# A graph-attention and hypergraph kernel on one core: a second buffer for the transposed adjacency, one transpose placed earlier on VectorE, two prologue vectors in borrowed buffers

## The chip, the core and the metric

The kernel runs on one core of one Trainium2 chip. The time is the device time of one execution in microseconds (us). The core has a matrix engine (TensorE, PE in the profile; the loading of its weights has a row of its own, PEld), a vector engine (VectorE, DVE), a scalar engine (ScalarE, ACT), a general engine (GpSimd, POOL) and an engine that issues transfers (SyncE, SP). [...]

## What is computed

There are 128 graphs of 128 nodes with 512 features each, all in fp32. Layer 0 is graph attention with 8 heads, then a residual and a layer norm. Layer 1 is two hypergraph convolutions with a ReLU and a layer norm between them, then residuals and a layer norm. Cut to what matters here:

```python
# layer 0: attention, 8 heads of 64
feats = einsum('bnf,hfu->bhnu', X, W)
dense = leaky_relu(e_self[..., :, None] + e_neigh[..., None, :], 0.2)
dense = dense + NEG_BIG * (1.0 - A[:, None])
out   = relu(softmax(dense) @ feats + b)
x     = layernorm(x + out)
# layer 1: two hypergraph convolutions (w1 512->1024, w2 1024->512)
def hypergraph_conv(x, adj, W, b):
    H  = (adj != 0)
    Dn = 1 / (H @ adj[first row]);  Be = 1 / H.sum(axis=1)
    m  = Be * (H^T @ (x @ W^T))
    return Dn * (H @ m) + b
h = layer_norm(relu(hypergraph_conv(x, adj, W1, b1)))
x = layernorm(x + hypergraph_conv(h, adj, W2, b2) + x)
```

## The kernel before

**Tiling.** Two graphs make a pair, and 64 pairs are worked through. Everything of a pair lies with the 128 nodes or 128 features across the partitions. The propagator `R`, the product H·Be·H^T scaled by Dn, is made once for each graph (`propagator`, L432, into the PSUM tile `pd`; `r_evict`, L440) and used in both convolutions. The large products are done by a scheme with seven products instead of eight, so TensorE's results of one product are added to others by VectorE and ScalarE: `chain` lists the products in the order 1, 2, 6, 5, 7, 4, 3. They go into three PSUM banks: X, Y and W. Product 5 opens bank W; VectorE's `y_sum` then adds a copy of X to W; and only after that may product 3 add into the same bank W. For the second weights this is `pyX`, `pyY`, `pyW` (multiplied at L476), the sums are L924, and ScalarE's copies of X are L332. For the first weights the names are `phX`, `phY`, `phW` (L840), with sums at L855.

**Pipeline.** A pair passes through stages that are spread over five periods ("lags" 0 to 4). In one period TensorE works at the second convolution of one pair, the features and attention of another, and the first convolution of a third. The period is 38.6 units in the planner's reckoning. Each function carries a lag and a due time; all functions of all pairs are sorted by `(pair + lag) * 38.6 + due` and written out in that order, which becomes the order on every engine's queue. So a due time is only a place in a queue, not a time at which anything runs.

**VectorE's order around the change.** In this stretch of a period VectorE's queue holds, with due times: `attended_pair` (26.3, L724 and L725, attention results to `y`), `sum_blocks` (28.9, L939 to L944, sums for the middle layer norm), `residual` of graph 0 (29.0, L739, `y <- max(y,0)+x`, then its statistics L747 and L748), `y_sum` for bank Y (30.6, L924), `residual` of graph 1 (30.7), `rstds` (30.8, L753), `x_transpose` of graph 1 (30.85, L373), `y_sum` for bank W (33.9, L924 again), `edges` (35.75, L409 to L416), `largest` (36.1, L601), a further `y_sum` on bank W (0.1 of the next period), `r_evict` (L440). GpSimd adds the bias to `y` ahead of the residuals (`add_bias`, L730, two instructions), takes the reciprocal root after `rstds` (L755), and masks the scores (L579). ScalarE then normalizes `y` (`first_output`, L782), which TensorE multiplies by `R` (`propagate`, L805, tile `pz`); ScalarE copies that out (`z_evict`, L817, tile `zT`).

**`x_transpose`** turns 32 x 32 blocks of a pair's x, loaded blockwise as `xb` by four transfers, into `xT`, one instruction for each graph (the first half due 26.15, the second 30.85). `xT` is read by the feature products in the following period.

**`edges`** transposes the adjacency blocks `ab` into `hT`, compares with zero and counts degrees. `hT` is one buffer: `edges` of pair p stands in the queues ahead of `propagator` of pair p-1, which still reads `hT` of pair p-1, so the first instruction of `edges` waits for that product:

```python
hT = work.tile([P, 2, N], F32, tag="hT", name=f"hT_{p}")   # one buffer
@step(0, 35.75)   # edges, of pair p
@step(1, 40.1)    # propagator, of pair p - 1: 1.5 units into the next period
```

**Prologue.** The attention vectors `as_bc` and `an_bc` are spread over the partitions by two transfers from ScalarE's queue at the very start and read by `prepare_first` (L222). The tag `eb` holds two larger buffers for the exponentials on their way to the transpose (`e_read`, L621).

Of the kernel before, what the change touches and what calls it, by code (L numbers as in the profile page):

```python
# [8 lines left out]
F32 = mybir.dt.float32  # L9
# [11 lines left out]
def kernel(  # L21
# [46 lines left out]
    G, N, F = x.shape  # L68
    P = 128
# [13 lines left out]
    const = ctx.enter_context(tc.tile_pool(name="const", bufs=1))  # L83
    work = ctx.enter_context(tc.tile_pool(name="work", bufs=1))
# [72 lines left out]
    def everywhere(t, ap, queue):  # L157
        queue.dma_start(t, ap.partition_broadcast(P))

    as_bc, an_bc, b0_bc, b2_bc, bw_bc = (  # L160
        const.tile([P, F], F32, name=n) for n in ("as_bc", "an_bc", "b0_bc", "b2_bc", "bw_bc")
    )

    vecs = const.tile([P, 3, KH], F32, name="vecs")
# [139 lines left out]
    def step(lag, time, since=0, until=PAIRS):  # L304

        def keep(fn):
            steps.append((lag, time, fn.__name__, range(since, until), fn, ()))
            return fn
        return keep

    def at(lag, time, fn, *args, since=0, until=PAIRS):
        steps.append((lag, time, fn.__name__, range(since, until), fn, args))
# [63 lines left out]
        )  # L376

    at(0, 26.15, x_transpose, 0, since=2)
    at(0, 30.85, x_transpose, 1, since=2)

    def x_transpose_first(p, s):
        s["px"] = [bank(f"px_{p}_{g}") for g in range(2)]
# [17 lines left out]
    @step(0, 35.75)  # L400
    def edges(p, s):

        deg = small.tile([P, 2], F32, tag="deg", name=f"deg_{p}")
        hT = work.tile([P, 2, N], F32, tag="hT", name=f"hT_{p}")
        if p < 2:
            src = s["pt"][:, :2 * N].rearrange("p (g n) -> p g n", g=2)
        else:
            src = hT
            nc.vector.transpose(hT.rearrange("p g (b n) -> p (g b) n", b=NB), s["ab"])  # L409
        for g in range(2):  # L410
            nc.vector.tensor_scalar(
                hT[:, g, :], src[:, g, :], 0.0, None, op0=ALU.not_equal, op1=ALU.add,
                accum_out=deg[:, g:g + 1],
            )
        nc.vector.tensor_scalar(deg, deg, 1.0, None, op0=ALU.max)
        nc.vector.reciprocal(deg, deg)  # L416
        s["hT"], s["be"] = hT, deg
# [65 lines left out]
    def feature(s, i, to, start):  # L483
# [4 lines left out]
          feature, FW, since=2)  # L488
# [772 lines left out]
```

## Time and profile before

| quantity | value |
|---|---|
| time, median of 3 runs | 2449.46 us (2448.19 to 2449.68) |
| span of the profiled execution | 2448.5 us |
| TensorE matmul / weight loads busy | 2419.9 us / 2146.3 us |
| VectorE, ScalarE, GpSimd busy | 1906.3, 1528.1, 1803.8 us |
| HBM traffic | 239.08 MB read, 102.73 MB written |

The page gives each engine's busy time, then the chain that ended last, then groups of instructions by line with the idle time just ahead of them and what ended it. Idle time of an engine matters only if somebody whom the end depends on waits behind it.

A timeline lists instructions in order of their start: start, duration, engine, line, operation, output and inputs, shapes, count, and in brackets the idle time before it and what ended that. Several like instructions are merged in one line; durations on TensorE overlap, so the distance between two starts is the better measure there. TensorE's work of a period, from one `pd` to the next, takes about 37.4 us.

### The profile page before, as it was taken

Reading aid. Unit: us, or ns where it says so; the run is one execution under the profiler, and the core shown is the slowest. Engines: PE = TensorE matmul, PEld = TensorE weight load, DVE = VectorE, ACT = ScalarE, POOL = GpSimd, SP = SyncE. Lnnn points to the kernel's source line nnn. Section 1 sums busy time; section 2 is a strip of 40 time slices with the busy share of each in tenths; the row PEclk is TensorE's granted clock in tenths of the full one; section 3 lists DMA queues with packets and bytes.
Section 4 is the critical chain, followed back from the end, with each engine's and each line's share of the span. In section 5 each row is a group of like instructions: output and inputs, shape, how many; then the busy total and the mean of one; then the engine's idle time right before and its main releaser. Section 6 shows DMA issues by size and latency. Waiting matters only on the chain.

```text
span 2448.5 us, 52709 instructions
## 1 busy us (share of the span) xinstructions
PE 2419.9 (99%) x18273; PEld 2146.3 (88%) x18273; DVE 1906.3 (78%) x4456; ACT 1528.1 (62%) x4481; POOL 1803.8 (74%) x2060
## 2 busy tenths in 40 slices
PE   7999999999999999999999999999999999999998
PEld 5888888888888888888888888888888888888897
DVE  7877778778778777787787787777877877877776
ACT  4665765756756657657567566576575675665763
POOL 5777776777777777777777777777777777777774
PEclk9999999999999999999999999999999999999999
DMA  6545445445455454454454554554544545545531
GB/s 184 138 139 151 144 132 150 144 134 148 140 144 147 136 154 140 135 151 142 135 145 145 142 147 140 149 148 129 153 136 139 150 139 147 144 138 152 144 112 52
DMA packets 432762, 345.30 MB, mean 141 GB/s; under 512 B 153176, under 2 KB 382064, under 8 KB 432496
## 3 DMA queue, kind: packets, MB, share of 16 engines
q1 hardware_dynamic: 429024, 337.46, 48.4%
q10 hardware_dynamic: 3472, 4.47, 0.5%
q8 instruction: 145, 2.38, 0.4%
q14 instruction: 121, 0.99, 0.1%
HBM read 239.08 MB, written 102.73 MB: 140 GB/s over the span
## 4 chain that ended last, share of the span: by engine, by line
PE 96%; DVE 2%; DMA 1%; ACT 1%; issue 0%; POOL 0%; SPq 0%; POOLq 0%; DVEq 0%; ACTq 0%
PE phX L840 19%; PE pyX L476 18%; PE pyW L476 9%; PE phW L840 9%; PE pfX L476 9%; PE pav L693 5%; PE pz L805 5%; PE phY L840 5%; PE pfW L476 4%; PE pq L1006 4%; PE pyY L476 4%; PE pfY L476 2%; PE pd L432 1%; PE pf L513 1%; PE py L1052 0%
## 5 line engine op out<-in xcount | busy, mean ns | idle before, releaser
L332 ACT COPY py<-pyX 128x257 f32<-128x257 f32 x189 | 70.8, 375 | 531.2 <-PE pyX L476 526.7
L840 PEld LDWEIGHTS phX<-zS,w_sb 128*128 128x128 f32 x3072 | 362.8, 192 | 41.3 <-issue 31.4
L840 PE MATMUL phX<-zS,w_sb 128*128 128x128 f32 x3072 | 378.8, 276 | 2.2 <-POOL xS L458 1.3
L893 POOL TENSOR_TENSOR sq<-sq 128x512 f32<-128x512 f32 (+2 forms) x384 | 329.6, 858 | 20.3 <-ACT sq L881 0.3
L579 POOL TENSOR_TENSOR nb<-nb,neg 128x512 f32<-128x512 f32 x256 | 318.0, 1275 | 7.5 <-DMA nb<-rd 7.3
L595 ACT ACTIVATE nb<-nb,ft 128x128 f32<-128x128 f32 x1020 | 317.3, 390 | 6.8 <-POOL nb L579 6.8
L755 POOL TENSOR_TENSOR rso<-veo,mhalf 128x2 f32<-128x2 f32 x63 | 44.2, 702 | 372.4 <-DVE veo L753 372.4
L609 ACT ACTIVATE nb<-nb,nm 128x128 f32<-128x128 f32 x1024 | 313.8, 394 | 0.4 <-DVE nm L601 0.4
L870 ACT ACTIVATE h<-h,vecs 128x128 f32<-128x128 f32 x768 | 245.5, 395 | 29.7 <-DVE h L855 29.7
L476 PE MATMUL pyW<-w_sb,hS 128*128 128x256 f32 x1008 | 243.9, 384 | 2.5 <-DVE y L924 2.2
L476 PE MATMUL pyX<-w_sb,hS 128*128 128x257 f32 x1008 | 245.6, 385 | 0.0
L476 PE MATMUL pyX<-w_sb,h 128*128 128x257 f32 x1008 | 239.2, 379 | 0.5 <-ACT py L332 0.5
L409 DVE STREAM_TRANSPOSE hT<-ab 128x256 f32<-128x256 f32 x62 | 27.6, 445 | 264.2 <-PE pd L432 264.2
L476 PEld LDWEIGHTS pyW<-w_sb,hS 128*128 128x128 f32 x1008 | 186.2, 189 | 44.1 <-issue 17.7
L476 PEld LDWEIGHTS pyX<-w_sb,h 128*128 128x128 f32 x1008 | 190.9, 190 | 29.0 <-ACT py L332 0.9
L476 PEld LDWEIGHTS pyX<-w_sb,hS 128*128 128x128 f32 x1008 | 185.8, 189 | 28.7
L499 DVE TENSOR_TENSOR ft<-pf,pfW 128x264 f32<-128x264 f32 x124 | 53.2, 429 | 170.3 <-PE pfW L476 89.4
L601 DVE TENSOR_REDUCE nm<-nb 128x4 f32<-128x512 f32 x256 | 169.2, 681 | 7.0 <-ACT nb L595 6.0
L630 DVE STREAM_TRANSPOSE eT<-eb 128x512 f32<-128x512 f32 x252 | 163.5, 687 | 0.6 <-DMA eb<-ed 0.5
L881 ACT ACTIVATE sq<-h 128x512 f32<-128x512 f32 x256 | 160.4, 627 | 2.1
L730 POOL TENSOR_TENSOR y<-y,b_bc 128x512 f32<-128x512 f32 x128 | 160.1, 1272 | 1.9 <-DVE y L704 1.5
L458 POOL TENSOR_TENSOR hS<-h 128x512 f32<-128x512 f32 x126 | 158.9, 1282 | 2.3 <-ACT h L870 2.3
(178 smaller groups left out, 5810.3 us busy)
## 6 DMA issues: line engine op xcount, KB each, us to landing
nb<-rd SPq DMA_DIRECT2D x127, 512.0 KB
ed<-nb SPq DMA_DIRECT2D x126, 512.0 KB
eb<-ed SPq DMA_DIRECT2D x504, 128.0 KB
x<-in_x_dram SPq DMA_DIRECT2D x64, 512.0 KB
out_dram<-o SPq DMA_DIRECT2D x63, 512.0 KB
xb<-in_x_dram SPq DMA_DIRECT2D x248, 128.0 KB
a<-in_adj_dram SPq DMA_DIRECT2D x64, 128.0 KB
w<-in_adj_dram SPq DMA_DIRECT2D x128, 64.0 KB
```

The source lines that it names most:

```text
L458: engine.tensor_tensor(t[:, i], in0, in1, op=op)
L476: nc.tensor.matmul(to[:, :n], lhs[:, k, :], rhs[:, k, :n], start=bool(start) and k == 0, stop=(k == nk - 1), skip_group_check=True,)
L579: nc.gpsimd.tensor_tensor(t, t, neg[:, :, None, :].to_broadcast([P, NB, HH, B]), op=ALU.add)
L595: nc.scalar.activation(t, t, AF.Prelu, bias=s["ft"][:, g, h, 0:1], alpha=SLOPE)
L601: nc.vector.tensor_reduce(s["nm"][:, g, hs], scores(p, s, g, hs).rearrange("p b h j -> p h b j"), AX.XY, ALU.max, negate=True,)
L609: nc.scalar.activation(t, t, AF.Exp, bias=s["nm"][:, g, h:h + 1])
L630: nc.vector.transpose(s["eT"][:, g, hs, :].rearrange("p h (b i) -> p h b i", b=NB), s["eb", g][:, :, hs, :].rearrange("p b h j -> p h b j"),)
L730: nc.gpsimd.tensor_tensor(s["y"][:, g, :], s["y"][:, g, :], b0_bc, op=ALU.add)
L840: nc.tensor.matmul(to[:, m * N:(m + 1) * N], w[:, k, m * P:(m + 1) * P], rhs[:, k, :], start=bool(start) and m == 0 and k == 0, stop=(k == ...
L870: nc.scalar.activation(dst[:, k, :], src[:, k, :], AF.Relu, bias=b1_sb[:, c:c + 1])
L881: nc.scalar.activation(s["sq"][:, g, q * KH // 2:(q + 1) * KH // 2, :], hid(s, g, q), AF.Square, scale=DH ** -0.5,)
L893: nc.gpsimd.tensor_tensor(t[:, :n, :], t[:, :n, :], t[:, n:2 * n, :], op=ALU.add)
```

## The change

The tag `hT` gets two buffers. The second half of `x_transpose` gets the due time 28.95 instead of 30.85. This puts it behind `sum_blocks` and ahead of both `residual` functions instead of behind `rstds`. For pair 2 an explicit table sets both transposes' places, which stay as they were; for pairs 0 and 1 another function makes `xT`. The vectors `as_bc` and `an_bc` are taken from the tag `eb` in the pool `work` instead of having buffers of their own in `const`.

```diff
-    as_bc, an_bc, b0_bc, b2_bc, bw_bc = (
-        const.tile([P, F], F32, name=n) for n in ("as_bc", "an_bc", "b0_bc", "b2_bc", "bw_bc")
+    as_bc, an_bc = (
+        work.tile([P, F], F32, tag="eb", name=n, bufs=2) for n in ("as_bc", "an_bc")
+    )
+    b0_bc, b2_bc, bw_bc = (
+        const.tile([P, F], F32, name=n) for n in ("b0_bc", "b2_bc", "bw_bc")
     )
...
     at(0, 26.15, x_transpose, 0, since=2)
-    at(0, 30.85, x_transpose, 1, since=2)
+    at(0, 28.95, x_transpose, 1, since=2)
...
-        hT = work.tile([P, 2, N], F32, tag="hT", name=f"hT_{p}")
+        hT = work.tile([P, 2, N], F32, tag="hT", name=f"hT_{p}", bufs=2)
```

In the order of the built programs, no instruction is added or removed on any engine. On VectorE the second `x_transpose` stands ahead of eight instructions (L739, L747, L748, L924, L739, L747, L748, L753) that it followed before, once per period; the transpose into `hT` (L409) no longer carries a wait on TensorE; the next `y_sum` on bank W and `r_evict` (L440) carry it instead, each for its own input. The orders on GpSimd, ScalarE, TensorE and SyncE are the same; on TensorE one wait on its own earlier work stands at the first `pfY` product instead of the first `pfX`.

## The prediction

> **What bounds the kernel now.** I read the busy times and the chain of waits first.
>
> ```profile
> PE 2419.9 (99%) x18273; PEld 2146.3 (88%) x18273; DVE 1906.3 (78%) x4456; ACT 1528.1 (62%) x4481; POOL 1803.8 (74%) x2060
> PE 96%; DVE 2%; DMA 1%; ACT 1%; issue 0%; POOL 0%; SPq 0%; POOLq 0%; DVEq 0%; ACTq 0%
> ```
>
> TensorE sets the end; from one `pd` to the next it takes a median 37.39 us. An edit on VectorE is worth only what it takes out of TensorE's row. Next, the waits, VectorE's and TensorE's:
>
> ```profile
> DVE hT L409 <- PE pd L432: 264.2, 61, 4.4
> PEld pyW L476 <- issue: 17.7, 61, 0.5
> PE pyW L476 <- DVE y L924: 2.2, 2, 2.0
> ```
>
> The largest wait (4.3 us a period) is the one for the single `hT` buffer, but it is VectorE's own. The second row is small, unexplained ("issue") and regular: 61 times, 0.29 us, before a weight load for `pyW`. The third names VectorE's L924 at that place. So I read one period there, TensorE and then VectorE:
>
> ```profile
> 1211.79 1.89 PE L476 MATMUL pyW<-w_sb,hS 128*128 128x256 f32 x8
> 1213.52 1.89 PE L476 MATMUL pyX<-w_sb,h 128*128 128x256 f32 x8
> 1215.33 1.97 PE L476 MATMUL pyW<-w_sb,hS 128*128 128x256 f32 x8
> 1217.14 1.95 PE L805 MATMUL pz<-R,y 128*128 128x128 f32 x16
> ...
> 1209.36 1.51 DVE L739 SCALAR_TENSOR_TENSOR y<-y,x 128x512 f32<-128x512 f32 x1
> 1210.90 0.69 DVE L747 BATCH_NORM_STATS2 statsa<-y 128x6 f32<-128x512 f32 x1
> 1212.04 0.69 DVE L739 SCALAR_TENSOR_TENSOR y<-y,x 128x512 f32<-128x512 f32 x1
> 1213.70 0.17 DVE L753 TENSOR_SCALAR vea<-mva 128x2 f32<-128x2 f32 x1
> 1213.78 1.11 DVE L373 STREAM_TRANSPOSE xT<-xb 128x512 f32<-128x512 f32 x1
> 1214.80 0.39 DVE L924 TENSOR_TENSOR y<-py,pyW 128x256 f32<-128x256 f32 x1
> 1219.57 0.45 DVE L409 STREAM_TRANSPOSE hT<-ab 128x256 f32<-128x256 f32 x1 [4.38 <-PE pd L432]
> ```
>
> Groups of eight `py` products start 1.73 us apart (1211.79 to 1213.52); the next two distances are 1.81 and 1.81. L924 ends at 1215.19 and the weights of the last `pyW` group load at 1215.30: product 3 adds into the bank that L924 still reads. L373, the transpose that the change moves, stands right ahead of that L924. The last period with this pattern has no L373, since there is no further pair:
>
> ```profile
> 2372.99 1.89 PE L476 MATMUL pyX<-w_sb,h 128*128 128x256 f32 x8
> 2374.72 1.89 PE L476 MATMUL pyW<-w_sb,hS 128*128 128x256 f32 x8
> 2376.45 1.95 PE L805 MATMUL pz<-R,y 128*128 128x128 f32 x16
> ...
> 2373.26 0.42 DVE L924 TENSOR_TENSOR y<-py,pyW 128x256 f32<-128x256 f32 x1 [0.51 <-PE pyW L476]
> ```
>
> There both distances are 1.73 and the period is 37.25 us. The second 0.075 us belongs to the same wait: a weight load that waited no longer overlaps the products before it.
>
> [...] 99% busy hides the 0.14 us a period above. [...] the first L739 (two inputs) takes 1.51 us beside GpSimd's second L730, which ends at 1210.33; the second L739 takes 0.69; L373 (one input) takes 1.15 beside GpSimd and 1.09 elsewhere. [...] after a stop of some 2.2 us at 89 to 91 us the `pz` products lie 0.213 us apart, not 0.11.
>
> **The change, part by part.**
>
> *The transpose ahead of the residuals.* L373 issues no DMA and goes ahead of eight VectorE instructions. It starts at 1209.36; its follower starts 1.02 us later (1213.78 to 1214.80), at 1210.38. By then L730 has ended (1210.33), so the first L739 takes 0.69 us and its follower starts at 1210.38 + 0.72 = 1211.10, against 1210.90: everything from there to L753 is 0.20 us later, because the transpose fills the time in which the residual was held. L924 follows L753 at once: 1213.98 to 1214.37. With the 0.11 us seen above, TensorE could load at 1214.48; it wants to at 1213.52 + 1.73 - 0.21 = 1215.04. Margin 0.56 us, so the wait goes. In the 60 periods from 96.6 us on that have L373, the first distances sum to 4.6 us more than 60 x 1.731 and the second to 4.5 more than 60 x 1.732 (three periods lose 0.2 to 0.3 extra, within the margin). Gain 9.1 us.
>
> *What is queued behind the 0.20 us.* GpSimd's L755, ScalarE's L773 to L782. L782 for graph 0 ends 1215.88 + 0.20 = 1216.08; `pz` loads at 1216.93 - 0.14 = 1216.79. ScalarE's copies then end at 1218.21, the first `zT` copy starts there, the second is due when `pz` is done, 1219.12 - 0.14 = 1218.98, and ScalarE is free for it at 1218.69. GpSimd's four L579 end about 0.2 later, and `zS` has over 1 us before its product. All of this lies beside TensorE: cost zero.
>
> *The first such period (54 to 97 us)* lacks margin: the groups at 87.46, 91.35 and 93.84 us take 3.89, 2.49 and 2.75 us instead of 1.73, 1.73 and 1.78. VectorE reaches L739 only at 85.18, and L924 ends at 91.21. With the transpose first L739 waits for L730's end (86.38) as before, and L924 comes 0.99 us earlier. At least 0.97 us is won; if the shorter stop does not drop the clock, another 0.69 + 0.96, so 2.6. Stops of 1.1 and 1.3 us at 61 to 64 us left the clock up. ScalarE then limits it: L922 ends at 94.07, so its second `zT` copy can start 0.48 us later, at about 94.5 instead of 96.79. I take 2.1.
>
> *Two buffers for `hT`.* VectorE's 61 waits, 264.2 us, go. TensorE gains nothing by it: behind L409 stand L601, L924, L440, L963 and L855, whose results TensorE needs at 1228.4 at the earliest (L996 ends at 1226.37). L924 and L440 now wait on TensorE for `pyW` and `pd`, some 2 us earlier than they run now. Queued behind them are L963, whose input transfers are issued from 1216.31 to 1218.89, and L601 and L855, which need ScalarE and `phY` at 1223; nobody gets later. The `ab` transfers are issued until 1203.3; their landing is not shown, but a late one would be hidden until 1219.57. Bounds: nothing below, since VectorE takes the same order earlier; above, 0.21 us a period if the other regular loss moved (the `ph` groups at 1224.73 and 1226.65 take 1.92 and 1.86 us for 1.79). I take 0: that one waits for ScalarE's copy L332 at 1225.94, ahead of which ScalarE is busy without a break from its second `zT` copy on.
>
> *The two vectors.* Read for the last time at 13.9 us; the tag's next transfer is issued at 64.3. Same transfers, same queue: 0, hidden by 50 us of other work.
>
> Sum: 9.1 + 2.1 = 11.2 us from the span of 2448.5, so 2437.3. The timed runs' median is 1.0 above that span: **2438.3 us**.
>
> **The rivals.**
> - *Both losses go* (chance 0.04). If VectorE's earlier L601 freed ScalarE, the `ph` loss went too: 61 x 0.21 = 12.8 more, 2425.5. For: L601 feeds ScalarE's L609. Against: ScalarE has no gap there.
> - *Half a gain* (0.11). L924 is earlier but the `pyW` wait only shrinks, or the first period wins just 1 us: 3 to 8 us, about 2444.
> - *It does nothing* (0.05): the 0.29 us are TensorE's own dispatch. Against: the period without L373. 2449.
> - *Slower: the residuals are late* (0.10). If the first L739 still takes 1.51 us, everything to L753 is 1.02 us later. ScalarE's second `zT` copy could then start at 1218.01 + 1.02 + 0.48 = 1219.51 instead of 1218.98, and as ScalarE has no gap from there to L332, TensorE pays 0.53 us, less the 0.14 won: 60 x 0.39 = 23, about 2472. It decides from 0.63 us on; above 0.49 it eats the gain. For: L739 is held in nearly every period. Against: L730, which holds it, ends before L739 would start.
>
> **How the numbers follow.** The main case has chance 0.70: 2435 to 2441, from the first period's bounds and a few tenths either way. 0.2% of the time, 4.9 us, is about what a measurement of this kernel can tell from no change. Faster by more: 0.70, 0.04 and two thirds of the half gain, 0.81. The same: the rest of that and 0.05, 0.09. Slower: 0.10. The range, 2435 to 2446, takes in the main case and most of the half gain.
>
> **What would show it.** Right: the `pyW` row of 61 "issue" waits is gone, both distances are 1.73 us, a period is 37.25 us, the first L739 takes 0.69, the `hT` wait is gone, and ScalarE's `zT` copies still wait on `pz`. Wrong: the first L739 still at 1.51, or a new wait at `phX` or `pz`.

## The result and the profile after

The changed kernel takes 2439.2 us (median of 4 runs, 2437.71 to 2441.57) against 2449.57 us (4 runs, 2448.19 to 2450.67): 10.4 us less, a ratio of 0.9959 with a 95% interval of 0.9942 to 0.9976. The forecast was 2438.3. The profiled execution has a span of 2435.9 us, 12.6 under that of before; the profiled run of after is the fastest of its four, so the spans lie further apart than the medians. All its lines from the diff on carry slightly higher numbers: L373 is L376, L739 is L742, L924 is L927, L409 is L412, L476 is L479, L817 is L820.

The busy times and the chain of the profile after, from its page:

```profile
PE 2408.6 (99%) x18273; PEld 2148.9 (88%) x18273; DVE 1931.5 (79%) x4456; ACT 1523.3 (63%) x4481; POOL 1795.8 (74%) x2060
PE 97%; DVE 1%; DMA 1%; ACT 1%; issue 0%; POOL 0%; SPq 0%; POOLq 0%; DVEq 0%; ACTq 0%
```

TensorE still sets the end, and its row has lost 11.3 us. The waits of VectorE, and then of the weight loads (engine and line, the thing waited for, us in total, times, longest):

```profile
DVE nm L604 <- ACT nb L598: 120.2, 94, 3.0
...
DVE so L966 <- DMA sums_out<-sd: 56.9, 52, 2.4
DVE R L443 <- PE pd L435: 23.6, 57, 1.2
...
PEld phX L843 <- issue: 31.6, 127, 1.3
PEld pav L696 <- issue: 21.4, 62, 0.3
...
PEld pyW L479 <- issue: 1.4, 1, 1.4
```

The wait for `hT` is gone. VectorE waits instead for ScalarE's scores, for the transfer of the sums and for `pd`, some 200 us in all. The `pyW` row, 61 times before, is down to one: the first period.

One period of the timeline, TensorE and then VectorE (lines that do not bear on the argument are left out, here and below):

```profile
1203.78 1.89 PE L479 MATMUL pyW<-w_sb,hS 128*128 128x256 f32 x8
1205.51 1.89 PE L479 MATMUL pyX<-w_sb,h 128*128 128x256 f32 x8
1207.24 1.89 PE L479 MATMUL pyW<-w_sb,hS 128*128 128x256 f32 x8
1208.97 1.95 PE L808 MATMUL pz<-R,y 128*128 128x128 f32 x16
...
1201.36 1.09 DVE L376 STREAM_TRANSPOSE xT<-xb 128x512 f32<-128x512 f32 x1
1202.35 0.67 DVE L742 SCALAR_TENSOR_TENSOR y<-y,x 128x512 f32<-128x512 f32 x1
1205.85 0.17 DVE L756 TENSOR_SCALAR vea<-mva 128x2 f32<-128x2 f32 x1
1205.93 0.42 DVE L927 TENSOR_TENSOR y<-py,pyW 128x256 f32<-128x256 f32 x1
1206.27 0.44 DVE L412 STREAM_TRANSPOSE hT<-ab 128x256 f32<-128x256 f32 x1
```

All groups of eight now start 1.73 us apart. The first residual, L742, takes 0.67 us for 1.51. L927 starts 0.42 us after the `pyX` group (1205.51), against 1.28 us before (1214.80 after 1213.52).

Where the span's 12.6 us come from, by the starts of the `pd` products in both traces:

| stretch | before, us | after, us | difference |
|---|---|---|---|
| start to `pd` of pair 1 | 54.44 | 53.40 | -1.04 |
| to `pd` of pair 2 | 42.14 | 39.47 | -2.67 |
| the next 61 periods | 2281.64 | 2272.77 | -8.87 |
| the end | 70.24 | 70.26 | 0.02 |

The median period went from 37.39 to 37.26 us. The first line is chance: `pd` of pair 0 starts at 24.6 us in the profile after and 25.5 before, and anywhere from 25.1 to 27.0 in the other profiles below, 26.2 in a second profile of the changed kernel itself.

### The profile page after: what moved, and what is told of

It reads as the page before. It is cut to its first block, busy times and chain, and to the rows that moved or that the text cites. A ratio compares the mean times of both kernels' runs of the same rounds, so it can differ in the third digit from the quotient of the medians.

```text
span 2435.9 us, 52769 instructions
## 1 busy us (share of the span) xinstructions
PE 2408.6 (99%) x18273; PEld 2148.9 (88%) x18273; DVE 1931.5 (79%) x4456; ACT 1523.3 (63%) x4481; POOL 1795.8 (74%) x2060
## 4 chain that ended last, share of the span: by engine, by line
PE 97%; DVE 1%; DMA 1%; ACT 1%; issue 0%; POOL 0%; SPq 0%; POOLq 0%; DVEq 0%; ACTq 0%
PE phX L843 19%; PE pyX L479 18%; PE phW L843 9%; PE pfX L479 9%; PE pyW L479 9%; PE pav L696 5%; PE pz L808 5%; PE phY L843 5%; PE pfW L479 5%; PE pq L1009 4%; PE pyY L479 4%; PE pfY L479 2%; PE pd L435 1%; PE pf L516 1%; PE py L1055 0%
## 5 line engine op out<-in xcount | busy, mean ns | idle before, releaser
L479 PE MATMUL pyX<-w_sb,hS 128*128 128x257 f32 x1008 | 245.6, 385 | 0.0
L479 PE MATMUL pyX<-w_sb,h 128*128 128x257 f32 x1008 | 239.2, 379 | 0.5 <-ACT py L335 0.5
L479 PE MATMUL pyW<-w_sb,hS 128*128 128x256 f32 x1008 | 238.6, 378 | 1.0 <-DVE y L927 1.0
L479 PEld LDWEIGHTS pyX<-w_sb,h 128*128 128x128 f32 x1008 | 190.9, 190 | 29.0 <-ACT py L335 0.9
L479 PEld LDWEIGHTS pyW<-w_sb,hS 128*128 128x128 f32 x1008 | 190.6, 189 | 28.8 <-issue 1.4
L479 PEld LDWEIGHTS pyX<-w_sb,hS 128*128 128x128 f32 x1008 | 185.7, 189 | 28.7
L733 POOL TENSOR_TENSOR y<-y,b_bc 128x512 f32<-128x512 f32 x128 | 160.3, 1273 | 2.4 <-DVE y L707 1.1
L999 DVE SCALAR_TENSOR_TENSOR y<-y,rsh,bw_bc 128x512 f32<-128x512 f32 x126 | 148.3, 1215 | 11.7 <-POOL rsh L995 8.9
```

Source lines behind the costliest of these rows:

```text
L479: nc.tensor.matmul(to[:, :n], lhs[:, k, :], rhs[:, k, :n], start=bool(start) and k == 0, stop=(k == nk - 1), skip_group_check=True,)
L733: nc.gpsimd.tensor_tensor(s["y"][:, g, :], s["y"][:, g, :], b0_bc, op=ALU.add)
```

## The experiments

My theory was that the whole lasting gain is L924 no longer standing behind the transpose. The rivals gave it to the second `hT` buffer, to the prologue vectors, or to the filling of the time in which the first residual is held beside GpSimd (1.51 us, against 0.69 for the second). Each time is compared with the kernel before on the same chip (2450.6, 2450.5, 2450.7 and 2451.0 us).

**The three parts apart.** The transpose alone (before, with this edit):

```diff
-    at(0, 30.85, x_transpose, 1, since=2)
+    at(0, 28.95, x_transpose, 1, since=2)
```

> The transpose of the second half at 28.95, one hT buffer, vectors in their old place. My theory (the gain is L924 no longer standing behind the transpose, and the hT buffer is worth nothing): the period 37.25 us, both distances around the last pyW group 1.73 us, hT still waiting 4.3 us a period for the propagator; the time 10 to 11 us under before, about 2439. Rival A (the 264 us of hT waits are what the change gains by): less than a third of the gain, 2446 or more. The first period is the open point: with one hT buffer edges still waits for pd there, which itself comes earlier; at most 1 us of the 2.4 could be missing.

Measured: 2440.61 us, ratio 0.9958 (0.9943 to 0.9973), median period 37.26 us. The wait for the single `hT` is larger than before and costs nothing. From the waits of VectorE of this kernel:

```profile
DVE hT L409 <- PE pd L432: 278.9, 56, 5.1
```

The two `hT` buffers and the vectors, without the transpose (after, with `28.95` set back to `30.85`):

> Two hT buffers and the two vectors in the eb buffers, the transpose at its old place 30.85. My theory: VectorE's wait of L409 for pd is gone and L440 and L924 run some 2 us earlier, yet the period stays 37.39 us and the time 2449 (within 1.5 us of before). Rival A: most of the gain, 2443 or less. Rival B (VectorE's earlier score maxima also free ScalarE, so the ph loss of 0.21 us a period goes): 2437.

Measured: 2450.86 us, ratio 1.0003 (0.9994 to 1.0012), period 37.39 us. Its timeline in the period where the residual took longest (1.75 us), VectorE and TensorE:

```profile
1215.40 1.08 DVE L376 STREAM_TRANSPOSE xT<-xb 128x512 f32<-128x512 f32 x1
1216.41 0.38 DVE L927 TENSOR_TENSOR y<-py,pyW 128x256 f32<-128x256 f32 x1
1216.71 0.44 DVE L412 STREAM_TRANSPOSE hT<-ab 128x256 f32<-128x256 f32 x1
...
1214.56 1.89 PE L479 MATMUL pyX<-w_sb,h 128*128 128x256 f32 x8
1216.94 1.97 PE L479 MATMUL pyW<-w_sb,hS 128*128 128x256 f32 x8 [0.48 <-DVE y L927]
```

`hT` is written at once, 3.9 us earlier in the period (2.15 us after the start of `pyX` instead of 6.05), but L927 still stands behind the transpose and TensorE behind L927. Here the profile names the wait that it calls "issue" elsewhere. Rivals A and B fall.

The vectors alone (before, with the first part of the diff):

> Only the two vectors in the eb buffers. My theory: nothing, 2449 within the noise of about 1.5 us. Rival C (the prologue, which was 1.0 us shorter in the profile of after, is shortened by this part): pd of pair 0 at 24.6 us instead of 25.5 in the profile, and 1 us less in the time.

Measured: 2450.5 us, ratio 0.9999 (0.999 to 1.0008); `pd` of pair 0 at 25.1 us. Rival C falls.

**Ahead, or only away?** In before, the transpose behind L924 instead of ahead of the residuals:

```diff
-    at(0, 30.85, x_transpose, 1, since=2)
+    at(0, 34.0, x_transpose, 1, since=2)
```

> Before, with the transpose of the second half behind L924 (due 34.0) instead of ahead of the residuals; one hT buffer, old vectors. It fills none of the time in which the first L739 is held, so L739 stays at 1.51 us. My theory (only L924's place behind the transpose cost TensorE time): period 37.25 us and about the time of after, 2439 to 2440, with L924 ending about 0.2 us earlier than in after. Rival D (the gain needs the transpose to fill the time in which the residual is held by GpSimd): no more than half the gain, 2444 or more.

Measured: 2440.82 us, ratio 0.9959 (0.9944 to 0.9974), period 37.25 us. VectorE's timeline:

```profile
1203.98 1.48 DVE L739 SCALAR_TENSOR_TENSOR y<-y,x 128x512 f32<-128x512 f32 x1
1208.41 0.42 DVE L924 TENSOR_TENSOR y<-py,pyW 128x256 f32<-128x256 f32 x1
1208.75 1.10 DVE L373 STREAM_TRANSPOSE xT<-xb 128x512 f32<-128x512 f32 x1
```

The residual takes as long as ever (1.48 us) and the gain is the same; L924 starts 0.13 us earlier against `pyX` than in after (median). So filling that time is not what pays; that L924 does not stand behind the transpose is.

**The margins.** After, with the transpose made a second time at its old place, which delays L924 and not the residuals:

```diff
     at(0, 28.95, x_transpose, 1, since=2)
+    at(0, 30.85, x_transpose, 1, since=3)
```

> After, with the transpose of the second half made a second time at its old place (same data written again), so that L924 is 1.02 us later than in after while the residuals are not. My theory (L924 has 0.56 us of margin at TensorE): TensorE's last pyW group starts 0.27 us late and its weight load no longer overlaps, 0.075 more: 0.345 a period, 21 us over 60 periods and 1 to 2.6 in the first: about 2461. Rival F (the loss at pyW is TensorE's own): no change from after, 2439.

Measured: 2459.04 us, ratio 1.0037 (1.0022 to 1.0051). Against the period of after, a period is 37.53 for 37.26 us, 0.27 and not 0.345 longer. In TensorE's timeline:

```profile
1218.40 1.89 PE L480 MATMUL pyX<-w_sb,h 128*128 128x256 f32 x8
1220.33 1.97 PE L480 MATMUL pyW<-w_sb,hS 128*128 128x256 f32 x8
1222.14 1.95 PE L809 MATMUL pz<-R,y 128*128 128x128 f32 x16
```

The distances are 1.93 and 1.81: 0.20 us of waiting and 0.075 for the weights. I had expected 0.27 and 0.075; the reckoning from a margin and a fixed part stands here, the first part was taken 0.07 too long. In after L927 starts 0.40 us behind the start of `pyX` (median), not 0.46 as forecast, and the second transpose delays it by 1.00 us while the weight load comes 0.38 us late: the margin is 0.62 us and not 0.56. Rival F falls.

After, with one ScalarE copy of 128x512 into an unused tile at the end of `first_shift`, so ahead of `first_output` (extra work, nothing left out):

```diff
+        nc.scalar.copy(made["spare"], b0_bc)
```

> After, with one ScalarE copy of 128x512 into an unused tile ahead of L782 (extra work, nothing left out): ScalarE's chain from the residuals to the zT copies gets about 0.57 us longer. My theory of the slower rival (ScalarE's second zT copy has 0.3 us to spare and from there to L332 there is no gap): the copy is 0.27 us late, TensorE loses that in each of 61 periods ahead of the phX group that waits for L332, 16 us in all, about 2455. Rival E (ScalarE has idle time enough, 37% of the span): no change from after, 2439.

Measured: 2447.15 us, ratio 0.9987 (0.998 to 0.9994); the period is 37.33 us. So it costs 0.07 us a period and some 7 to 8 us over all, half of what I expected, but more than the nothing of rival E (2439.2 and 2439.83 us for the changed kernel were measured on other chips). ScalarE's timeline of after, then that of this kernel:

```profile
1209.81 0.35 ACT L925 COPY y<-pyX 128x256 f32<-128x256 f32 x1
1210.06 0.59 ACT L820 COPY zT<-pz 128x512 f32<-128x512 f32 x1
1210.96 0.59 ACT L820 COPY zT<-pz 128x512 f32<-128x512 f32 x1 [0.31 <-PE pz L808]
```

```profile
1213.89 0.60 ACT L782 COPY spare<-b_bc 128x512 f32<-128x512 f32 x1
1214.40 1.51 ACT L786 ACTIVATE y<-y,sh,rsa 128x512 f32<-128x512 f32 x2
1216.99 0.35 ACT L926 COPY y<-pyX 128x256 f32<-128x256 f32 x1
1217.24 1.06 ACT L821 COPY zT<-pz 128x512 f32<-128x512 f32 x2
```

The extra copy delays its follower by 0.51 us (1213.89 to 1214.40), though its duration reads 0.60. The spare time was larger too. Two `zT` copies without a gap start 0.48 us apart, and in after the second starts 0.90 us after the first: 0.42 us to spare, not the 0.31 that the bracket shows, since durations of neighbours overlap by some 0.1 us. So the second copy should be 0.51 - 0.42 = 0.09 us late; against the start of `pz` it is 0.07 us late in the median. TensorE loses 0.08 us, in the first `phX` group (1.87 us to the next start instead of 1.79).

**The other regular loss.** After, with one block of L595 (leaky scores) and its maximum behind ScalarE's second `phX` copy:

```diff
-        ((1, 0), 34.2, (2, 2.05), (2, 2.1), 7.8, 21.5), ((1, 1), 35.4, (2, 6.0), (2, 7.3), 7.9, 21.55),
+        ((1, 0), 34.2, (2, 2.05), (2, 2.1), 7.8, 21.5), ((1, 1), 35.4, (2, 7.55), (2, 7.6), 7.9, 21.55),
```

> After, with the fourth block of L595 (leaky of graph 1, heads 4 to 7) due 7.55 instead of 6.0 and its maximum due 7.6, so that ScalarE's second phX copy stands ahead of it, 1.17 us earlier. My theory (the remaining regular loss of 0.21 us a period at the ph groups is TensorE waiting for that copy): the groups at phW and phX start 1.79 us apart, period 37.05 us, 12 to 13 us less than after, about 2426.5. Rival F (these distances are TensorE's own way of changing tiles): no change, 2439. Rival G (the maximum and the exponential of that block come late and push the ed transfers): the loss reappears ahead of the pav group, 2439 or more.

Measured: 2428.81 us, ratio 0.9911 (0.9897 to 0.9926), period 37.04 us. In the traces only ScalarE's order of instructions differs from after; those of TensorE, VectorE, GpSimd and SyncE are the same. TensorE's timeline and the copy in ScalarE's, first of after, then of this kernel:

```profile
1216.56 1.95 PE L843 MATMUL phW<-zS,w_sb 128*128 128x128 f32 x16
1218.49 2.02 PE L843 MATMUL phX<-zS,w_sb 128*128 128x128 f32 x16
1220.35 1.89 PE L1009 MATMUL pq<-y,R 128*128 128x512 f32 x4
...
1216.61 1.27 ACT L598 ACTIVATE nb<-nb,ft 128x128 f32<-128x128 f32 x4
1217.78 0.57 ACT L335 COPY ph<-phX 128x512 f32<-128x512 f32 x1
```

```profile
1214.42 1.95 PE L843 MATMUL phW<-zS,w_sb 128*128 128x128 f32 x16
1216.20 1.95 PE L843 MATMUL phX<-zS,w_sb 128*128 128x128 f32 x16
1217.99 1.89 PE L1009 MATMUL pq<-y,R 128*128 128x512 f32 x4
...
1212.11 2.45 ACT L612 ACTIVATE nb<-nb,nm 128x128 f32<-128x128 f32 x8
1214.62 0.59 ACT L335 COPY ph<-phX 128x512 f32<-128x512 f32 x1
1215.10 1.28 ACT L598 ACTIVATE nb<-nb,ft 128x128 f32<-128x128 f32 x4
```

The distances are 1.79 and 1.79 instead of 1.92 and 1.86 (medians). In after the copy ends at 1218.35, 0.14 us before the `phX` group starts; here it ends 0.99 us before. Rivals F and G fall. But the stretch up to `pd` of pair 2 grew to 42.50 us. So the same edit, with pairs 0 and 1 left as they were:

```diff
-        at(lag, tl, leaky, g, q)
...
+        late = 2 if (g, q) == (1, 1) else 0
+        at(lag, tl, leaky, g, q, until=late or PAIRS)
...
+        if late:
+            at(2, 7.55, leaky, g, q, since=late)
...
```

> The previous order of L595 (fourth block and its maximum behind ScalarE's second phX copy) for pairs from 2 on, while pair 1 keeps the order of after. In the profile of the version for all pairs the stretch from pd of pair 1 to pd of pair 2 took 42.50 us where after has 39.47. My theory: that stretch comes back to about 39.5 (the prologue work of pair 1 was upset by the later maximum), the later periods stay at 37.04 us: 3 us less than the version for all pairs, about 2425.8. Rival H (the 3 us lie in the state of the clock and the transfers at the start and not in the order): no change from the version for all pairs, 2428 to 2429.

Measured: 2427.22 us (2426.59 to 2428.97), ratio 0.9908 (0.9891 to 0.9924); that stretch takes 39.69 us. The kernel before it had taken 2426.32 to 2429.01 on another chip, so this alone did not separate the two.

**Side by side on one chip.** The last four kernels settle two small points: what the second `hT` buffer is worth in the first period, and whether the order in pairs 0 and 1 matters.

> The changed kernel itself, on the same chip as the three kernels below, to compare with them. My theory: 10 to 11 us under before, ratio 0.9957. Rival I (the second hT buffer saves 1 us in the period from pd of pair 2, 37.5 us here against 38.5 in the profile with one buffer): 1 us faster than the version with one buffer.

> The transpose alone, one hT buffer, again. My theory: within 0.5 us of the changed kernel; the longer period from pd of pair 2 seen in its profile goes with transfers that landed late in that execution. Rival I: 1 us slower, and the period from pd of pair 2 is 38.5 us again.

> The later fourth block of L595 for all pairs, again. Theory (the order for pair 1 costs 3 us in the stretch up to pd of pair 2): 2 to 3 us slower than the next kernel, the stretch 42.5 us again. Rival H (that stretch varies from execution to execution): the same time within 0.7 us.

> The later fourth block of L595 from pair 2 on, again. Theory: 2 to 3 us faster than the kernel before this one in the list; rival H: the same within 0.7 us. Both: about 12 us faster than the changed kernel.

| kernel | time, us | ratio to before | period from `pd` of pair 2 |
|---|---|---|---|
| changed kernel | 2439.83 (2439.26 to 2440.92) | 0.9955 (0.9941 to 0.9969) | 37.52 |
| transpose alone, one `hT` | 2440.21 (2439.88 to 2441.69) | 0.9958 (0.9945 to 0.997) | 38.29 |
| later block, all pairs | 2429.81 (2429.57 to 2430.07) | 0.9914 (0.99 to 0.9927) | 37.34 |
| later block from pair 2 | 2427.82 (2427.53 to 2428.59) | 0.9906 (0.9892 to 0.9919) | 38.31 |

The second `hT` buffer: 0.4 us between the medians, with overlapping runs. The period from `pd` of pair 2 was longer in all three profiles with the moved transpose and one buffer (38.54, 38.34, 38.29) and 37.52 twice with two; but the last row has two buffers and 38.31. Whether the buffer is worth up to 1 us there stays open; nothing here points to more. The order in pairs 0 and 1: 2.0 us between the medians, runs apart, and the long stretch (42.50 us) came back: the order matters, rival H falls. The traces show where the time goes. With pair 1 in its old order TensorE stops twice between 61 and 68 us, for 0.7 to 1.3 us at a `phX` group that waits for ScalarE and for about 1.4 us at the next, which waits for GpSimd's `xS`. In both profiles of the version for all pairs it stops only at the second, for 2.6 us, and then the granted clock is 0.50 for 3.41 us, which costs about 1.7 us by estimate (half of 3.41). A further 1.1 us goes at the `pyW` group, where it stops for 2.3 us instead of 1.2.

The last kernel beats both: 23 us under before, 12 under the changed kernel.

## Why the prediction was right

- **The transpose out of L924's way, 9.1 us.** The 60 periods gave it: both distances are 1.731 us in the median, the sum of the excess was 9.08 and is zero. The transpose behind L924 gives the same and twice the transpose takes it back, so this is shown by runs both ways. The working held in its parts: L756 is 0.16 us later against TensorE than before (0.20 forecast), the residual 0.67 (0.69), L927 earlier by 0.86 (0.82).
- **What is queued behind the delay.** As forecast, ScalarE's second `zT` copy still waits for `pz` (0.31 us in the line above).
- **The first period, 2.1 us.** The stretch lost 2.67; `pd` and the first `phX` of the next took back 0.27 (0.62 and 1.89 us instead of 0.45 and 1.79, waiting for ScalarE, which was the limit named): 2.40 us. The stop at `pyW` fell from 2.16 to 1.20 us and the slow `pz` products did not come (from `pz` to `pd` 1.78 us instead of 2.75). The reason given for the latter, that stops of 1.1 and 1.3 us had left the clock up (they lie at 62 to 67 us, not at 61 to 64), looks at the length alone; in the section on the hardware stops of one length went either way. How much of the 2.4 us the other runs had is open: in the profile of the vectors alone the stop is as long as in before (2.17 us), the granted clock stays at 1.00, and the same stretch takes 40.99 us instead of 42.14, so 1.1 us less could be won. That the 2.1 came near is luck in part.
- **Two `hT` buffers, zero.** Shown: the buffers without the transpose give a ratio of 1.0003, the transpose without them 0.9958. 264 us of waiting were taken away and nobody was waiting behind them.
- **The vectors, zero.** Shown, 0.9999.
- **The slower rival.** It did not come, since the residual took 0.67 us. Its price was mis-sized: "It decides from 0.63 us on" let the first `zT` copy start where the duration of the copy before it ends. Start to start (0.48 us for a copy that reads 0.59), ScalarE has about 0.1 us more to spare, and the extra copy cost 0.07 us where this reckoning gave 0.27.
- **The forecast's 0.9 us too low** lies within the scatter: the 2439.83 of the second chip and this median differ by 0.6.
- **The remaining loss at `ph`** was put down to ScalarE's copy L332 and not to VectorE. Shown: two `hT` buffers left it, moving one ScalarE block, with every other engine's order unchanged, took it away, 12 us.

## What to carry to other kernels

A wait of 264 us that heads the list can be worth nothing and a row of 0.29 us without a named cause 9 us: compare the distances between the starts of like groups on the engine that sets the end, period by period, and look for a period where the suspect is absent. To cure it, move the instruction that stands in front of the one that is waited for; ahead or behind came to the same here (ratios 0.9958 and 0.9959), within the margins of the others. Reckon margins from start to start of neighbouring instructions, not from their durations (0.48 against 0.59 us at ScalarE's copies).

## What was not expected of the hardware

- A short wait on TensorE had a fixed part in these traces. In the places looked at where a weight load waited, the group that followed took 0.07 to 0.10 us longer, beyond the wait itself: 1.807 for 1.731 at `pyW`, 1.859 for 1.787 at `phX`, 1.87 for 1.787 with the late ScalarE copy, whose wait was otherwise too short to delay the group's start, and 1.889 at the first `phX` behind `pd` of pair 2 in after. At `pyW` it lies between the first and the second product of the group: 0.29 us for 0.215 in before.
- Stops of TensorE of nearly the same length, 2.14 to 2.17 us at `pyW`, were followed by half clock in three profiles and by full clock in one. In before the granted clock is 0.50 from 44.65 to 54.89 us and from 92.44 to 95.85 us, and 1.00 between and behind these until 2444.22 us: the second stretch lasts 3.41 us, the first 10.24, three times that, and the 37.55 us between them are eleven times that. So the traces were counted out in stretches of 3.41 us from a change of the clock. From 57 us on, in before and after, TensorE was busy for 1.42, 1.48 and 0.73 us in the three full-clock stretches ahead of half clock (the last two at the very end), and for 2.13 us or more in every other. The stops at `pyW`, by the emptiest stretch that each left:

| profile | stop at `pyW`, us | TensorE busy in the emptiest stretch, us | clock in the next |
|---|---|---|---|
| before | 2.16 | 1.42 | half |
| two `hT` buffers and vectors | 2.16 | 1.42 | half |
| transpose twice | 2.14 | 1.43 | half |
| vectors alone | 2.17 | 2.15 | full |
| later block, all pairs | 2.29 | 2.02 | full |
| later block, all pairs, second profile | 2.30 | 1.65 | full |

  The last two of these profiles have half clock behind the stops of 2.6 us at 63 to 67 us (1.40 and 1.04 us busy). The rows by stretch, of before and then of the vectors alone (stretch, length, busy time of PE, PEld, DVE, ACT and POOL with the number of instructions, granted clock, DMA share, GB/s):

```profile
89.02:92.43 3.41, 1.42 (x7) 1.01 (x6) 3.34 (x8) 1.87 (x5) 2.74 (x4) 1.00 0.24 59
92.44:95.85 3.41, 3.41 (x15) 3.06 (x14) 3.27 (x6) 1.69 (x7) 3.30 (x3) 0.50 0.40 146
...
87.31:90.72 3.41, 2.15 (x10) 1.52 (x9) 3.27 (x8) 0.20 (x1) 1.69 (x4) 1.00 0.23 55
90.73:94.14 3.41, 2.68 (x16) 2.50 (x17) 3.38 (x7) 3.28 (x9) 3.41 (x4) 1.00 0.51 169
```

  The stretch at half clock cost before 1.65 us: it takes 2.49 and 2.75 us for the two groups behind the stop, and the vectors alone take 1.81 and 1.78:

```profile
87.56 1.89 PE L479 MATMUL pyX<-w_sb,h 128*128 128x256 f32 x8
91.46 1.97 PE L479 MATMUL pyW<-w_sb,hS 128*128 128x256 f32 x8 [2.00 <-DVE y L927]
93.27 1.95 PE L808 MATMUL pz<-R,y 128*128 128x128 f32 x16
95.05 0.61 PE L435 MATMUL pd<-hT,hB 128*128 128x128 f32 x4
```

  In after, with its stop of 1.20 us, TensorE was busy for 2.37 us of the emptiest stretch there (87.42 to 90.83 us), and the clock stayed full.
- This part was expected: the first residual went from 1.51 to 0.67 us when the transpose went first, and GpSimd's L733 had ended at 1202.29, just before the residual started at 1202.35. The transpose itself took 1.09 us beside L733.
